# A DiT block on one core: where the sigmoid of the attention stage stands in ScalarE's order, and how one pair of modulation rows is ordered

## The chip, the cores and the metric

The kernel runs on one core of a Trainium2 chip. The metric is the device time of one execution in microseconds, the median of several runs. A core has five engines with an instruction stream each: TensorE (PE, matrix products), VectorE (DVE), ScalarE (ACT), GpSimd (POOL) and SyncE (SP, which here only issues transfers).

## What is computed

Two batches of 4096 rows of 512 numbers pass through one block with adaptive layer norms. Cut to what matters (the quantization rounds blocks of 16 numbers to an FP4 grid with a scale for each block):

```python
mod = (silu(c) @ wmod).reshape(2, 6, 1, -1)          # sa, ca, ga, sb, cb, gb
h = layernorm(x) * (1 + ca) + sa
xn = h / norm(h) * sqrt(d) * gamma
q, kv, a = split(xn @ W_qkva.T, 3)
a = sigmoid(a)
y[t] = a[t] * y[t-1] + kv[t]                         # scan along the rows
x = x + ga * (q * y)
h = layernorm(x) * (1 + cb) + sb
g, u = fp4_linear(h, w_gate), fp4_linear(h, w_up)    # 512 -> 1408
x = x + gb * fp4_linear(silu(g) * u, w_down)         # 1408 -> 512
```

## The kernel before

**Two stages.** The first (from line 778) does the gated scan and, beside it, the quantization of the three feed-forward weights. The second (from line 988) does the feed-forward part, 64 steps of 128 rows. Both have their order written out by hand: inside `tc.manual_schedule` each engine runs its instructions in the order in which the program issues them, so the order of the calls in the loop is the order on every engine's queue.

**The first stage** goes through 16 blocks of 512 rows (`NBLK`), each in four slots, one for each 128 of the 512 output features (`e`). Slot `s` stands for block `s // 4` and feature group `s % 4`; there are 64 slots and three more in which the last ones drain. The loop is at line 788. In a slot:

- TensorE runs `mix` (line 396): three products of 12 matmuls each (line 405) into three PSUM banks, in the order a, kv, q. Even slots use banks 0 to 2, odd ones 3 to 5. Operands are split in a high and a low half (`hl`), hence three passes.
- `gates` (line 415) takes the sigmoid of the product a on ScalarE, into the tile `sig`, which has one buffer. `scan` (line 420) runs along the rows on VectorE: it reads `sig` and the product kv, and writes `y`; ScalarE copies the last column to `cy` for the next block. `read_out` (line 430) multiplies by the product q. `halves` and `joined` (lines 437 and 446) split `y` for a transposing transfer and join it again, on ScalarE; `residual` (line 453) adds it to the rows on POOL and writes them to memory. All of these run a slot or more after `mix`: the loop keeps slot `s`'s products in `gate` and handles them in slot `s + 1`, `joined` and `residual` in slot `s + 3`.
- The rows of the next block are prepared, one group of 128 rows a slot: row group `g = slot + 4` is finished and `g + 1` begun. `norm_center` and `norm_shift` (VectorE, lines 166 and 172) apply the layer norm; `norm_square` (ScalarE, line 366) sums the squares, POOL makes the reciprocal root `rn` (`norm_gain`, lines 371 and 373); a slot later `norm_hi` (ScalarE, line 379) makes the high half and `norm_lo` (VectorE, line 384) the low half, and SyncE issues the transpose into `xT` (line 388). A block's first `mix` needs the four groups of its `xT`.
- Units of weight work, by the list `plan` (line 547), are loaded in one slot and handled in the next: the maxima of the weights' blocks in slots 6 to 22 (`weight_max`, line 479; two units a slot), their collection in 23 to 25, and their quantization in slots 26 to 59 (`quant`, line 97; one unit a slot, steps 1 to 6 spread over the slot). In the last slots the first row groups of the second stage get their statistics and quantization (`stats_x`, line 593; `quant_x`, line 606).

**ScalarE's order in a slot** is thus: the sigmoid of the slot before, `joined`, `norm_hi`, `cy`, `halves`, the unit's steps (among them `she` and `sle`), `norm_square` and the unit's first step.

**The opening** (`start`, line 659) is written out by hand too. The modulation rows are small products of two rows (`mod_rows`, line 230): each `s` of the pair gets its own 32 columns of the array by `tile_position`, and the k-steps of the `s` alternate. `start` calls it for the pair (1, 0) of batch rows at line 680, after two spread products (line 221) and before the first `mix`; the three others come in slot 10 (`MODS`), and are stored by `mod_store` (line 267) in slot 11.

Of the kernel before, what the change touches and what calls it, by code (L numbers as in the profile page):

```python
# [19 lines left out]
KC = D // P  # L20
# [23 lines left out]
def tile_adaln_block(  # L44
# [147 lines left out]
    wm = {}  # L192
# [34 lines left out]
            )  # L227
        return pm

    def mod_rows(*mods):  # L230

        pm = side((P, D))
        rows = [(s, slice(32 * n, 32 * n + B)) for n, s in enumerate(mods)]
        for k in range(KC):
            for s, at in rows:
                T.matmul(
                    pm[at, :],
                    sc[:, k, :],
                    wm[s][:, k, :],
                    start=k == 0,  # L240
                    stop=k == KC - 1,
                    tile_position=(0, at.start),
                )
        return pm, rows

    def mod_columns(s):
# [333 lines left out]
    mods = {}  # L580
# [78 lines left out]
    def start():  # L659
        a, b_, c_ = PARTS  # L660

        def load_mod_piece(s, k):
            S.dma_start(wm[s][:, k, :], wmod[k * P : (k + 1) * P, s * D : (s + 1) * D])

        load_mod(1, KC)
        norm_load(0)
        S.dma_start(gam, gamma.partition_broadcast(P))
        for k, then in enumerate((PARTS[0], PARTS[1], PARTS[2], None)):
            if then is None:
                norm_load(1)  # L670
            else:
                load_part(0, then)
            load_mod_piece(0, k)
        norm_load(2)
        norm_load(3)
        load_qkva(1)
        norm_load(KC)
        pc = mod_spread(1, 0)
        ps = mod_spread(0, 0)
        pair = mod_rows(1, 0)  # L680

        norm_moments(0)
        norm_stats(0)
        gamma_qkva(0, a, V)
        A.activation(ca[0], pc, AF.Copy, bias=1.0)
        square_qkva(0, a)
        gamma_qkva(0, b_, V)
        square_qkva(0, b_)
        inverse_qkva(0, a, a + 1)
        norm_center(0)  # L690
        gamma_qkva(0, c_, V)
        inverse_qkva(0, b_, b_ + 1)
        hi_qkva(0, a, True)
        square_qkva(0, c_)
        lo_qkva(0, a)
        inverse_qkva(0, c_, c_ + 1)
        hi_qkva(0, b_, True)
        norm_moments(1)
        norm_stats(1)
        lo_qkva(0, b_)  # L700
        A.copy(sa[0], ps)
        norm_center(1)
        hi_qkva(0, c_, True)
        norm_shift(0)
        norm_square(0)
        lo_qkva(0, c_)
        norm_gain(0, G)
        norm_shift(1)
        norm_square(1)
        norm_hi(0)  # L710
        norm_moments(2)
        norm_moments(3)
        norm_gain(1, G)
        norm_stats(2)
        norm_hi(1)
        norm_stats(3)
        norm_lo(0, xT)
        load_mod_piece(2, 0)
        norm_center(2)
        norm_shift(2)  # L720
        norm_square(2)
        norm_lo(1, xT)
        load_mod_piece(2, 1)
        load_part(2, a)
        norm_gain(2, G)
        norm_center(3)
        norm_shift(3)
        norm_square(3)
        norm_gain(3, G)
        norm_hi(2)  # L730
        gamma_qkva(1, a, V)
        norm_lo(2, xT)
        load_mod_piece(2, 2)
        load_part(2, b_)
        norm_hi(3)
        gamma_qkva(1, b_, V)
        square_qkva(1, a)
        square_qkva(1, b_)
        norm_lo(3, xT)
        load_mod_piece(2, 3)  # L740
        load_part(2, c_)
        norm_load(KC + 1)
        inverse_qkva(1, b_, a + 1)
        gamma_qkva(1, c_, V)
        mod_store(*pair)
        square_qkva(1, c_)
        hi_qkva(1, a, False)
        inverse_qkva(1, c_, c_ + 1)
        lo_qkva(1, a)
        hi_qkva(1, b_, True)  # L750
        norm_moments(KC)
        hi_qkva(1, c_, True)
        lo_qkva(1, b_)
        gamma_qkva(2, a, V)
        square_qkva(2, a)
        norm_stats(KC)
        lo_qkva(1, c_)
        norm_load(KC + 2)
        load_qkva(3)
        norm_center(KC)  # L760
        gamma_qkva(2, b_, V)
        square_qkva(2, b_)
        norm_shift(KC)
        norm_square(KC)
        norm_gain(KC, G)
        gamma_qkva(2, c_, V)
        square_qkva(2, c_)
        gain_qkva(0)
        norm_moments(KC + 1)
        inverse_qkva(2)  # L770
        norm_stats(KC + 1)
        for part in PARTS:
            hi_qkva(2, part, False)
            lo_qkva(2, part)
        gain_qkva(1)
        gain_qkva(2)
# [8 lines left out]
    with order:  # L785
        xT = new_xT()
        start()
        for slot in range(NS + 3):
            i, e = divmod(slot, KC)
            if e == 0 and slot < NS:  # L790
                if slot:
                    xT = nxT
                nxT = new_xT() if i + 1 < NBLK else None
            units, coming = coming, load_units(plan[slot]) if slot < len(plan) else []
            g = slot + KC
            if g + 3 < NT:
                norm_load(g + 3)
            cur = mix(i, xT, e) if slot < NS else None
            late = rows
            rows = None  # L800
            if slot == 0:
                cols = mod_columns(2)
            elif slot == MODS:
                rows = mod_rows(3, 4, 5)
            if gate is not None:
                gate = gates(*gate)
            if len(joining) == 2 or slot >= NS + 2:
                residual(*joined(*joining.pop(0)))
            if g < NT:
                norm_hi(g)  # L810
            if slot == 1:
                for part in PARTS:
                    square_qkva(3, part)
            if gate is not None:
                gate = scan(*gate)
            if slot == 1:
                signed_floor(gq, cols, atile([P, KC, B], F32, "mag"))
                prep_gain(0)
            if g + 2 < NT:
                norm_moments(g + 2)  # L820
            if gate is not None:
                gate = read_out(*gate)
            if g < NT:
                norm_lo(g, nxT)
            if gate is not None:
                joining.append(halves(*gate))
            if g + 2 < NT:
                norm_stats(g + 2)
            for u in units:
                u.advance(1)  # L830
            if g + 1 < NT:
                norm_center(g + 1)
            for u in units:
                u.advance(2)
                u.advance(3)
            if g + 1 < NT:
                norm_shift(g + 1)
                norm_square(g + 1)
            if slot == 1:
                scale_qkva(3)  # L840
                for part in PARTS:
                    hi_qkva(3, part, False)
                    lo_qkva(3, part)
            for u in units:
                u.advance(4)
            coming = [Unit(*c_) for c_ in coming]
            for u in coming:
                u.advance(0)
            if g + 1 < NT:
                norm_gain(g + 1, G)  # L850
            if slot == 0:
                for part in PARTS:
                    gamma_qkva(3, part, V)
            for u in units:
                u.advance(5)
                u.advance(6)
            assert all(u.step == 7 for u in units)
            if 0 < slot < KC:
                prep_gain(slot)
            if MODS - 5 <= slot < MODS - 2:  # L860
                load_mod(slot - MODS + 8)
            if late is not None:
                mod_store(*late)
            if slot == KC + 1:
                ca[1] = mod_load(1, 1, "mod_c1")
                sa[1] = mod_load(0, 1, "mod_s1")
            if slot == NS // 2 + KC:
                mods_for(0)
            if slot == NS // 2 + KC + 2:
                gbs[0] = mod_load(5, 0, "mod_gb")  # L870
            if slot in (NS - 6, NS - 5):
                for n in range(2):
                    n += 2 * (slot - NS + 6)
                    x1s[n] = load_x1(n)
            if NS - 5 <= slot < NS - 1:
                n = slot - NS + 5
                xst[n] = stats_x(x1s[n])
                if n in (1, 2):
                    run(quant_x(n - 1, x1s.pop(n - 1), xst.pop(n - 1)))
            gate = cur  # L880
# [190 lines left out]
```

## Time and profile before

| | us |
|---|---|
| median of 3 runs (1931.8 to 1933.85) | 1932.37 |
| the profiled execution | 1931.29 |
| its span, first to last instruction | 1929.5 |
| TensorE busy in the span | 1896.8 (98%) |
| VectorE busy | 1604.4 (83%) |
| ScalarE busy | 993.6 (51%) |
| POOL busy | 413.5 (21%) |

By stretch (busy us of each engine, granted clock of TensorE, mean share of the DMA engines):

| from, to | what | TensorE | VectorE | ScalarE | clock | DMA |
|---|---|---|---|---|---|---|
| 0 to 76.4 | opening, slots 0 to 3 | 57.36 | 53.61 | 36.08 | 0.89 | 0.84 |
| 76.4 to 244 | slots 4 to 23 | 159.75 | 130.31 | 83.97 | 1.00 | 0.78 |
| 244 to 555 | slots 24 to 63 | 311.00 | 283.84 | 230.78 | 1.00 | 0.91 |
| 555 to 1929.5 | second stage | 1368.65 | 1136.66 | 642.79 | 1.00 | 0.39 |

The lines of a profile are read so: in a timeline, start and length in us, the engine, the line of the kernel, the operation, what it writes and reads, how many; in brackets the idle time of the engine just before, and what ended it. "PEld" is the loading of weights into TensorE. In a list of waits: who waited for whom, the sum in us, how often, the longest. What ended a wait is inferred: where several conditions end close together, the last one is named.

### The profile page before, as it was taken

How to read it: one execution, taken by the hardware profiler on the slowest of the kernel's cores; microseconds unless marked ns; L12 is line 12 of the kernel's file. 1: busy time of each engine (PE TensorE's matmuls, PEld its weight loads, DVE VectorE, ACT ScalarE, POOL GpSimd, SP SyncE). 2: the span in 40 equal slices, each digit the busy share in tenths (PEclk: the TensorE clock that was granted, in tenths of full speed). 3: DMA queues.
4: the chain of work that ended last, by engine and by line, in shares of the span. 5: the costliest groups of instructions: out<-in, count | busy, mean ns of one | idle time of the engine just before them, and what ended most of it. 6: DMA issues, size and time to landing. Idle time of an engine off the chain costs nothing.

```text
span 1929.5 us, 25687 instructions
## 1 busy us (share of the span) xinstructions
PE 1896.8 (98%) x9220; PEld 899.4 (47%) x9220; DVE 1604.4 (83%) x2677; ACT 993.6 (51%) x1705; POOL 413.5 (21%) x597
## 2 busy tenths in 40 slices
PE   7899999999999999999999999999999999999999
PEld 4344444444444444444444444444444444444444
DVE  6778789999859988888888888878888888888865
ACT  4554577777755544444454445444544454444432
POOL 4544466666421010000000000001000000000000
PEclk8999999999999999999999999999999999999999
DMA  9796699999833444334433443344434333433333
GB/s 244 180 248 171 165 193 200 222 206 198 180 82 68 80 79 79 63 63 79 78 63 64 81 77 74 64 83 80 63 67 80 75 63 69 80 72 63 63 68 58
DMA packets 483202, 206.67 MB, mean 107 GB/s; under 512 B 439623, under 2 KB 440903, under 8 KB 483073
## 3 DMA queue, kind: packets, MB, share of 16 engines
q1 hardware_dynamic: 468624, 171.50, 41.9%
q0 software_dynamic: 14448, 33.52, 10.0%
q8 instruction: 72, 1.18, 0.3%
q14 instruction: 58, 0.47, 0.1%
HBM read 63.12 MB, written 33.58 MB: 50 GB/s over the span
## 4 chain that ended last, share of the span: by engine, by line
PE 84%; DVE 2%; issue 1%; ACT 1%; POOL 0%; DMA 0%; ACTq 0%; DVEq 0%; POOLq 0%
PE mm L898 46%; PE sd L945 24%; PE mm L405 15%; POOL xr L455 0%; DVE xn L122 0%; DVE ld L172 0%; DVE y L432 0%; DMA out_dram<-xr 0%; DVE y L423 0%; POOL out_dram L457 0%; DVE hl L125 0%; DVE ld L610 0%; DVE amx L147 0%; ACT she L113 0%; DVE hid L918 0%
## 5 line engine op out<-in xcount | busy, mean ns | idle before, releaser
L898 PEld LDWEIGHTS <-x2T 128*128 128x128 f16 x4608 | 450.9, 98 | 469.4 <-issue 1.3
L405 PE MATMUL mm<-xT,wqT 128*128 128x512 f16 (+1 forms) x2412 | 506.4, 374 | 21.0 <-DMA xT<-hl 12.6
L898 PE MATMUL mm<-wuT,x2T 128*128 128x512 f16 (+1 forms) x2304 | 487.7, 361 | 1.0 <-DVE hid L918 1.0
L898 PE MATMUL mm<-wgT,x2T 128*128 128x512 f16 (+1 forms) x2304 | 487.7, 361 | 0.0
L945 PE MATMUL sd<-wdT,hT 128*128 128x512 f16 x2112 | 465.8, 379 | 0.0
L405 PEld LDWEIGHTS <-wqT 128*128 128x128 f16 x2412 | 233.4, 100 | 294.8 <-issue 24.4
L945 PEld LDWEIGHTS <-hT 128*128 128x128 f16 x2112 | 206.6, 98 | 242.7
L913 ACT ACTIVATE silu<-mm,u 128x512 f32<-128x512 f32 (+1 forms) x192 | 125.1, 652 | 285.7 <-PE mm L898 281.9
L918 DVE SCALAR_TENSOR_TENSOR hid<-mm,u,silu 128x512 f32<-128x512 f32 (+1 forms) x192 | 128.4, 672 | 139.7 <-PE mm L898 130.6
L602 POOL TENSOR_SCALAR rstd<-vs 128x1 f32<-128x1 f32 x64 | 14.1, 221 | 983.9 <-ACT sq L600 983.9
L143 ACT ACTIVATE u<-ud,rms 128x1 f32<-128x1 f32 x64 | 19.0, 297 | 278.0 <-DVE rms L139 278.0
L120 ACT ACTIVATE sle<-sl 128x512 f16<-128x512 f32 (+2 forms) x162 | 147.2, 909 | 0.0
L113 ACT ACTIVATE she<-sh 128x1408 bf16<-128x1408 bf16 (+1 forms) x128 | 128.5, 1004 | 4.1
L969 POOL DMA_DIRECT2D out_dram<-o x63 | 56.2, 893 | 270.0 <-DVE o L963 266.1
L439 ACT COPY yh<-y 128x1024 uint16<-128x1024 uint16 x64 | 67.0, 1047 | 80.1 <-DVE y L432 70.7
L423 DVE TENSOR_TENSOR_SCAN y<-sig,cy,mm 128x512 f32<-128x512 f32 x56 | 71.6, 1279 | 43.3 <-POOL ss L371 19.3
L122 DVE SCALAR_TENSOR_TENSOR xn<-hid,xn 128x1408 f32<-128x1408 f32 x64 | 103.5, 1617 | 3.7 <-ACT hid L116 3.7
L106 DVE TENSOR_TENSOR xn<-hid,inv 128x1408 f32<-128x1408 f32 x64 | 104.0, 1625 | 2.2
L125 DVE SCALAR_TENSOR_TENSOR hhl<-hid,xn 128x1408 f16<-128x1408 f32 x64 | 104.0, 1625 | 2.2
L147 DVE TENSOR_REDUCE amh<-hid 128x88 f32<-128x1408 f32 x64 | 103.7, 1620 | 2.2
L116 ACT ACTIVATE hid<-xn 128x1408 f32<-128x1408 f32 x64 | 88.3, 1380 | 30.7 <-DVE xn L106 30.7
L455 POOL TENSOR_TENSOR xr<-xr,y 128x512 f32<-128x512 f32 x64 | 81.4, 1271 | 54.5 <-ACT y L447 53.7
(113 smaller groups left out, 1899.5 us busy)
## 6 DMA issues: line engine op xcount, KB each, us to landing
ld<-out_dram SPq DMA_DIRECT2D x65, 256.0 KB, 2.9
xr<-in_L_attn_x_dram SPq DMA_DIRECT2D x64, 256.0 KB, 3.4
out_dram<-xr POOLq DMA_DIRECT2D x64, 256.0 KB, 4.0
out_dram<-o POOLq DMA_DIRECT2D x63, 256.0 KB, 3.9
ld<-in_L_ffn_w_gate_dram SPq DMA_DIRECT2D x22, 256.0 KB, 3.2
ld<-in_L_ffn_w_up_dram SPq DMA_DIRECT2D x22, 256.0 KB, 3.2
ld<-in_L_ffn_w_down_dram SPq DMA_DIRECT2D x16, 256.0 KB, 3.0
scratch<-in_L_wmod_dram SPq DMA_DIRECT2D x12, 256.0 KB, 4.6
```

The costliest lines, as they stand in the source:

```text
L106: V.tensor_tensor(blocks(xn), blocks(src), spread(inv, nb), ALU.mult)
L113: A.activation(blocks(she), spread(sh, nb), AF.Copy, scale=WPEAK)
L116: A.activation(a, xn, AF.Abs, scale=MAGIC)
L120: A.activation(blocks(sle), spread(sl, nb), AF.Copy, scale=WPEAK)
L122: V.scalar_tensor_tensor(out=xn, in0=a, scalar=FLOOR, in1=xn, op0=ALU.max, op1=ALU.add)
L125: V.scalar_tensor_tensor(out=nq, in0=a, scalar=FLOOR, in1=xn, op0=ALU.max, op1=ALU.subtract)
L147: V.tensor_reduce(am, src.rearrange("p (b k) -> p b k", k=QB), AX.X, ALU.max, apply_absolute_value=True)
L405: T.matmul(pp[:, t : t + width], wqT[:, wp * KC + k, r * P : (r + 1) * P], xT[:, xp * KC + k, t : t + width], start=n == 0, stop=n == 3 * ...
L898: T.matmul(pp[:, : n1 - n0], x2T[:, xp * KC + k, :], wt[:, wp * KC + k, n0:n1], start=n == 0, stop=n == 3 * KC - 1,)
L913: A.activation(sl[:, :w], pairs[j][0][:, :w], AF.Silu, scale=u[:, 0:1])
L918: V.scalar_tensor_tensor(out=hid[:, n0:n1], in0=pairs[j][1][:, : n1 - n0], scalar=u[:, 1:2], in1=sl[:, : n1 - n0], op0=ALU.mult, op1=ALU.mult,
L945: T.matmul(pd, hT[:, hp * IC + k, :], wdT[:, wd_chunk(wp, k), :], start=n == 0, stop=n == 3 * IC - 1,)
```

## The change

`mod_rows` gets a switch that runs all k-steps of one row set before those of the next; only the opening's call uses it. In the loop, the sigmoid stays where it was up to slot 4. From slot 4 on (`KC` is 4) the sigmoid of the slot's own products is issued in that same slot, after steps 2 and 3 of the units and ahead of `norm_shift` and `norm_square` of the next rows; the next slot finds it done. In slot 4 both places are used, the old one for slot 3's products.

```diff
-    def mod_rows(*mods):
+    def mod_rows(*mods, one_by_one=False):
 
         pm = side((P, D))
         rows = [(s, slice(32 * n, 32 * n + B)) for n, s in enumerate(mods)]
-        for k in range(KC):
-            for s, at in rows:
-                T.matmul(
-                    pm[at, :],
-                    sc[:, k, :],
-                    wm[s][:, k, :],
-                    start=k == 0,
-                    stop=k == KC - 1,
-                    tile_position=(0, at.start),
-                )
+        steps = [(k, *r) for k in range(KC) for r in rows]
+        if one_by_one:
+            steps = [(k, *r) for r in rows for k in range(KC)]
+        for k, s, at in steps:
+            T.matmul(
+                pm[at, :],
+                sc[:, k, :],
+                wm[s][:, k, :],
+                start=k == 0,
+                stop=k == KC - 1,
+                tile_position=(0, at.start),
+            )
         return pm, rows
...
-        pair = mod_rows(1, 0)
+        pair = mod_rows(1, 0, one_by_one=True)
...
-            if gate is not None:
+            if gate is not None and slot <= KC:
                 gate = gates(*gate)
...
             for u in units:
                 u.advance(2)
                 u.advance(3)
+            if slot >= KC and cur is not None:
+                cur = gates(*cur)
             if g + 1 < NT:
                 norm_shift(g + 1)
                 norm_square(g + 1)
```

## Prediction

> **What bounds the kernel now.** TensorE is busy for 98% of the span, so only time in which it has no work can be won. I first ask where that is: the timeline of TensorE alone, with what ended each pause, and the chain of waits for the undisturbed rate.
>
> ```profile
> 76.41 31.24 PE L405 MATMUL mm<-xT,wqT 128*128 128x512 f16 x144 [2.56 <-DMA xT<-hl]
> 108.58 23.48 PE L405 MATMUL mm<-xT,wqT 128*128 128x512 f16 x108 [0.93 <-DMA xT<-hl]
> 131.99 3.61 PE L236 MATMUL sd<-scratch,sc 128*2 128x512 f32 x24
> 135.53 39.02 PE L405 MATMUL mm<-xT,wqT 128*128 128x512 f16 x180
> 176.58 31.24 PE L405 MATMUL mm<-xT,wqT 128*128 128x512 f16 x144 [2.02 <-issue]
> 210.43 31.24 PE L405 MATMUL mm<-xT,wqT 128*128 128x512 f16 x144 [2.62 <-DMA xT<-hl]
> 243.95 16.35 PE L405 MATMUL mm<-xT,wqT 128*128 128x512 f16 x75 [2.28 <-ACT y L447]
> ```
> ```profile
> 243.95 280.00 PE mm L405 x1296
> ```
>
> A slot is 36 matmuls, and 1296 in 280.00 us make 0.216 us each, 7.78 us a slot, 31.11 a block of four. Slot 4 starts at 76.41, slot 8 at 108.58, slots 16, 20 and 24 at 176.58, 210.43 and 243.95. All pauses stand where a block begins, and after 243.95 there is none until one of 1.03 us at 587. So slots 4 to 23 are short of something that isn't TensorE. Next I read one such boundary, slot 15 to 16, in the timeline of all engines:
>
> ```profile
> 172.01 0.74 DVE L384 SCALAR_TENSOR_TENSOR hl<-ld,rn,hl 128x512 f16<-128x512 f32 x1
> ...
> 172.82 1.29 SPq L388 DMA_TRANSPOSE xT<-hl  x1
> ...
> 175.85 0.74 DVE L172 SCALAR_TENSOR_TENSOR ld<-ld,rstd,sa 128x512 f32<-128x512 f32 x1
> 176.58 31.24 PE L405 MATMUL mm<-xT,wqT 128*128 128x512 f16 x144 [2.02 <-issue]
> 176.69 0.63 ACT L366 ACTIVATE sq<-ld 128x512 bf16<-128x512 f32 x1 [3.51 <-DVE ld L172]
> ...
> 177.32 0.67 ACT L417 ACTIVATE sig<-mm,us 128x512 f32<-128x512 f32 x1
> ...
> 178.08 1.28 DVE L423 TENSOR_TENSOR_SCAN y<-sig,cy,mm 128x512 f32<-128x512 f32 x1 [1.48 <-POOL ss L371]
> ```
>
> TensorE starts the block 3.76 us after SyncE issued the last transpose into xT (3.96 and 3.93 at the next two boundaries, so "issue" and "y L447" name the same wait), and that issue follows VectorE's norm_lo. VectorE sets the pace: scan to scan is 8.50 us, 0.72 more than TensorE's slot. In each slot it is idle for 1.48 us ahead of the scan: shift, then ScalarE's square, then the sigmoid behind it in ScalarE's order (177.32 + 0.67 = 177.99), then the scan at 178.08. ScalarE itself had idled 3.51 us ahead of the square, and the sigmoid's product was long there. The list of waits between 76 and 245 us adds them up:
>
> ```profile
> DVE y L423 <- POOL ss L371: 19.3, 13, 1.5
> ...
> DVE y L423 <- ACT sig L417: 7.1, 5, 1.5
> ```
>
> POOL's ss is no operand of the scan and ended at 177.73; it is the sigmoid in both lines, 18 waits of 1.48.
>
> [...] the sigmoid, ready, starts only after the square. [...] Here the granted clock is 0.50 between 25 and 30 us, behind a pause of 4.72. [...] 16 passes of the opening pair take 3.60 us, a pair of them each 0.43 us, and the spread rows' full-array passes take 0.43 each.
>
> **The change, part by part.**
> **1. The sigmoid ahead of the square, slots 4 to 24.** Nothing is added; 0.67 us of ScalarE goes from behind the square into the 3.51 us of idleness ahead of it. The scan can follow the shift at once, so VectorE's slot becomes 8.50 - 1.48 = 7.02 us. What is late next: norm_hi. Square, POOL's two operations and hi take some 2.5 us from the square's start, against 2.4 from the scan to norm_lo: 0.15 us more, 7.17 us. That is below 7.78, so TensorE becomes the bound and the pauses go. Then read_out starts 0.1 us after the product's end, norm_lo 0.65 later, the transpose's issue 0.81 later, its landing 3.95 later: 5.5 us into a slot of 7.78, 2.3 to spare.
> Start to start, the blocks took 176.58 - 135.53 = 41.05 (180 matmuls: 38.89), 33.85 and 33.52 (31.11 each): excess 2.16 + 2.74 + 2.41 = 7.31 us, all taken as won. Slot 8's excess is 32.17 - 31.11 = 1.06, but there the transpose was issued at 101.78 and landed 6.8 us later, behind a modulation load and three tiles issued from 98.77 on. Norm_lo comes only 0.5 us sooner (read_out then waits for the product's end, 99.75). Bounds 0 and 1.06; I take 0.2.
> **2. The wait that is added.** The sigmoid of slot s now stands on ScalarE from mid-slot until the first third of slot s's product is there, 2.6 us into it. Behind it: square, and through it POOL's ss and rn, norm_hi, norm_lo and the transpose. But norm_lo stands behind read_out of the whole product, 5.2 us later, so the wait can't be the last. It bites in slot 11: the modulation rows delay its product by 3.54, the square by some 1.5, and with it the copies of mod_store and VectorE. VectorE is then 1.9 us late at slot 12 and gains 0.6 a slot: level by slot 15. At nothing; cover gone, up to 1.5 us. `sig` has one buffer, but the scan that frees it is earlier in the same slot.
> **3. Slots 26 to 59.** VectorE needs 7.56 to 7.78 us a slot here and the scan hardly waits (L129 ends at 350.98, the scan starts at 351.03). The sigmoid falls between she/sle and the square, which starts 0.1 to 0.5 later; the two steps of a unit that VectorE does next don't need it. No gain, no loss.
> **4. The end of the stage, slots 59 to 63.** The sigmoid now precedes the statistics and quantization of the first rows on ScalarE. In slot 60 these start at 525.79 today; behind a sigmoid that waits until 526.7 for its third of the product and takes 0.6 they start at 527.3, 1.45 later with a small overlap. In slot 61 the third is there (534.4), and 0.6 is added. It is caught up before the last scan, which waits for TensorE anyhow:
>
> ```profile
> 552.56 1.28 DVE L423 TENSOR_TENSOR_SCAN y<-sig,cy,mm 128x512 f32<-128x512 f32 x1 [4.33 <-PE mm L405]
> ```
>
> 2.05 against 4.33: nothing. Cover gone, 2.05 us. The gap of 1.03 at 587 stays. No DMA issue and no POOL instruction is moved in its queue.
> **5. The opening pair one by one.**
>
> ```profile
> 16.93 3.60 PE L236 MATMUL sd<-scratch,sc 128*2 128x512 f32 x16
> 25.25 6.98 PE L405 MATMUL mm<-xT,wqT 128*128 128x128 f16 x72 [4.72 <-DMA xT<-hl]
> ```
>
> No tile runs beside another now: 16 x 0.43 = 6.9 us, ending at 23.8 in place of 20.5, ahead of xT at 25.25, 1.4 us to spare. The clock may then stay full from 25 us on; the rows after that wait for their own xT at 33.60 and 36.14, and the product of slot 3 waits 4.13 us for wqT at 63.19. So neither a faster start nor up to 2 us of a slower one counts: 0, bounds -0.3 and +0.5.
>
> **Sum.** 7.31 + 0.2 = 7.5 us. The profiled execution took 1931.29 us, its span 1929.5 and 1.8 around it: 1923.8. It lies 1.08 below the median of 1932.37; from the median, **1924.8 us**.
>
> **The rivals.**
> A. *The transposes land late.* With 167.6 us of that stretch at a DMA share of 0.78 squeezed into 160, the share is 0.82, and landing could take slot 8's 6.8 us in place of 3.95: 0.1 + 0.65 + 0.81 + 6.8 = 8.36, 0.58 over the slot at three boundaries. 1.75 us lost: 1926.6. Against it: between 300 and 500 us the share is 0.98 and TensorE never pauses.
> B. *The end of the stage shows* (part 4 without its cover): 2.05 lost, 1926.9.
> C. *It does not do what it says*: POOL releases the scan, as the list of waits has it, and VectorE stays at 8.50: 1932.4. Against it: ss ends 0.35 before the scan starts, the sigmoid 0.09.
> D. *Slower: VectorE becomes the bound in slots 26 to 59.* Its shortest slot is 7.56, 0.22 under TensorE's. If the sigmoid, put ahead of the square, delays VectorE by more than 0.22 + 7.5/34 = 0.44 us a slot, 34 slots eat the gain. Its whole 0.67 passed on would be 34 x 0.45 = 15.3, net 7.8 slower: 1940. For it: VectorE is 97% busy there. Against it: norm_hi of the next slot has idle room, as in part 3.
>
> **How the numbers follow.** Likeliest 0.68 (own range 1922.9 to 1926: all of slot 8's excess and the gap of 1.03 won at one end), A 0.13, B 0.08, C 0.06, D 0.05. Range 1922.9 to 1927.9, which leaves out C, D and the tail of B. 0.2% is 3.9 us, about what a measurement of this kernel can tell from no change. Likeliest, A and B are faster, 0.89; C the same, 0.06; D slower, 0.05.
>
> **What would show it.** Right: slots 16, 20 and 24 starting 31.1 us apart without a pause, slot 16 38.9 us after slot 11, the scan's 1.48 waits gone in slots 5 to 23, waits of VectorE for TensorE in their place, the span to slot 24 7.5 us shorter, and everything after it merely shifted. Wrong: pauses for xT still at the boundaries (A), a pause over 1.03 us around 580 (B), 1.48 still ahead of the scan under another name (C), pauses of TensorE between 244 and 520 us (D), or a first product later than 25.3.

## The result and the profile after

The changed kernel takes **1926.4 us** (median of 9 runs, 1925.1 to 1928.68); the kernel before, beside it on the same chip, 1933.57 (9 runs, 1931.8 to 1934.45). The ratio is 0.9966, with an interval of 0.9955 to 0.9976, so between 4.6 and 8.7 us are won. (One of the 13 runs of an experiment below, e2_pair_only, took 2001.41 us at a granted clock of 0.947 and is not among those that its ratio compares.)

The profiled execution took 1928.68 us, the slowest of the nine, with a span of 1926.9. Against the profiled execution of before (1931.29) only 2.6 us show. Three terms make them up, and the first two differ in sign, so the timeline of TensorE has to be read in parts. In the kernel after, two lines were added ahead of `mix`, so its matmul is L407, and the other lines up to the loop are two further down as well:

```profile
77.70 32.93 PE L407 MATMUL mm<-xT,wqT 128*128 128x512 f16 x144 [3.62 <-DMA xT<-hl]
111.43 23.48 PE L407 MATMUL mm<-xT,wqT 128*128 128x512 f16 x108 [0.80 <-DMA xT<-hl]
...
138.39 39.02 PE L407 MATMUL mm<-xT,wqT 128*128 128x512 f16 x180
177.65 84.53 PE L407 MATMUL mm<-xT,wqT 128*128 128x512 f16 x389 [0.24 <-issue]
```

The pauses of 2.02, 2.62 and 2.28 us ahead of slots 16, 20 and 24 are gone; 0.24 is left at slot 16, and this view shows none after it. With the second stage's first matmul at 551.11 (554.85 before), the terms are, from start to start:

| stretch | before | after | difference |
|---|---|---|---|
| up to slot 8 | 108.58 | 111.43 | +2.85 |
| slots 8 to 10 | 26.95 | 26.96 | 0 |
| slots 11 to 15 | 41.05 | 39.26 | -1.79 |
| slots 16 to 63 | 378.27 | 373.46 | -4.81 |
| the pause early in the second stage | 1.03 | 2.17 | +1.14 |

The stretch that the change aims at, slot 8 to the end of the stage, is 6.59 us shorter. The 2.85 ahead of it are the opening of this one execution: slot 4 starts 1.3 us later, after a pause of 3.62 in place of 2.56, and its block of 144 matmuls takes 32.93 in place of 31.24, at a granted clock of 0.79 between 76 and 84 us (1.00 before). In the experiments below the start of slot 8 moves between 108.4 and 112.5 us.

What VectorE waits for now is told by the list of waits between 76 and 245 us:

```profile
DVE y L434 <- ACT cy L428: 12.4, 14, 0.9
...
DVE y L425 <- PE mm L407: 6.9, 4, 3.9
...
DVE y L425 <- ACT sig L419: 1.2, 1, 1.2
```

The 18 waits of 1.48 ahead of the scan have become one of 1.2. But only 4 waits of the scan for TensorE took their place. There are 14 new ones of 0.88 ahead of `read_out` (L434). The timeline of all engines around one of them, slot 13's products:

```profile
158.25 0.68 ACT L419 ACTIVATE sig<-mm,us 128x512 f32<-128x512 f32 x1
...
161.68 1.27 DVE L425 TENSOR_TENSOR_SCAN y<-sig,cy,mm 128x512 f32<-128x512 f32 x1
...
162.49 1.15 ACT L449 COPY y<-yt 128x1024 uint16<-128x1024 uint16 x1
...
163.58 0.72 ACT L381 ACTIVATE hl<-ld,rn 128x512 f16<-128x512 f32 x1
...
164.21 0.18 ACT L428 COPY cy<-y 128x1 f32<-128x1 f32 x1
164.42 0.75 DVE L434 SCALAR_TENSOR_TENSOR y<-mm,gq,y 128x512 f32<-128x512 f32 x1 [0.88 <-ACT cy L428]
...
169.59 1.27 DVE L425 TENSOR_TENSOR_SCAN y<-sig,cy,mm 128x512 f32<-128x512 f32 x1
```

The sigmoid is ready at 158.93, and the scan follows the shift without a wait. `read_out`, however, writes over the `y` whose last column ScalarE's small copy `cy` reads, so it must come after that copy. `cy` takes 0.18 us, but stands in ScalarE's order behind the square, the copy of `joined` (1.15) and `norm_hi` (0.72). VectorE's slot is 169.59 - 161.68 = 7.91 us: 0.59 less than before, not 1.48 less. From the scan at 185.40 on most slots are shorter, 7.71 to 7.76 (8.30 to 8.35 before). Over the ten slots from 153.78 to 232.06 the mean is 7.83 (8.42 before), so VectorE and TensorE, whose slot is 7.78, run almost level.

### The profile page after: what moved, and what is told of

The parts are those of the page before. It is cut to its first block, busy times and chain, and to the rows that moved or that the text cites. A ratio compares the mean times of both kernels' runs of the same rounds, so it can differ in the third digit from the quotient of the medians.

```text
span 1926.9 us, 25653 instructions
## 1 busy us (share of the span) xinstructions
PE 1897.6 (98%) x9220; PEld 898.6 (47%) x9220; DVE 1604.6 (83%) x2677; ACT 997.3 (52%) x1705; POOL 413.7 (21%) x597
## 4 chain that ended last, share of the span: by engine, by line
PE 92%; DVE 3%; DMA 1%; ACT 1%; issue 1%; POOL 1%; SPq 0%; ACTq 0%; POOLq 0%; DVEq 0%
PE mm L902 46%; PE sd L949 24%; PE mm L407 22%; DMA scratch<-in_L_attn_W_qkva_dram 1%; DMA xT<-hl 1%; DVE hl L330 0%; POOL xr L457 0%; DVE y L434 0%; DVE ld L172 0%; POOL rs L303 0%; ACT sq L299 0%; DVE xn L122 0%; PE sd L238 0%; ACT yh L441 0%; DVE hl L324 0%
## 5 line engine op out<-in xcount | busy, mean ns | idle before, releaser
L407 PE MATMUL mm<-xT,wqT 128*128 128x512 f16 (+1 forms) x2412 | 506.1, 373 | 15.6 <-DMA xT<-hl 11.3
L407 PEld LDWEIGHTS <-wqT 128*128 128x128 f16 x2412 | 232.4, 99 | 290.1 <-issue 21.6
L106 DVE TENSOR_TENSOR xn<-hid,inv 128x1408 f32<-128x1408 f32 x64 | 104.0, 1625 | 2.2
L122 DVE SCALAR_TENSOR_TENSOR xn<-ld,xn 128x512 f32<-128x512 f32 (+1 forms) x98 | 67.0, 683 | 28.9 <-ACT ld L116 28.7
```

The costliest lines, as they stand in the source:

```text
L106: V.tensor_tensor(blocks(xn), blocks(src), spread(inv, nb), ALU.mult)
L122: V.scalar_tensor_tensor(out=xn, in0=a, scalar=FLOOR, in1=xn, op0=ALU.max, op1=ALU.add)
L407: T.matmul(pp[:, t : t + width], wqT[:, wp * KC + k, r * P : (r + 1) * P], xT[:, xp * KC + k, t : t + width], start=n == 0, stop=n == 3 * ...
```

## The experiments

Theory T: the place of the sigmoid ahead of the square is the whole gain; TensorE becomes the bound; `cy`'s wait takes some of the margin; the end of the stage gives about 1 us back. Rivals: the pair's order has a part in it (P), a transfer holds what is left (A), the end of the stage costs the 2 us that were priced (B), and VectorE is what limits slots 26 to 59 (D). Each diff is against the changed kernel, and every kernel computes the whole reference. All were timed in five rounds beside the kernel before; medians of different groups may be compared through the ratios only.

| kernel | us | ratio to before | interval | slot 8 starts | slot 8 to second stage | pause in second stage |
|---|---|---|---|---|---|---|
| before | 1933.57 | 1 | | 108.58 | 446.27 | 1.03 |
| the change | 1926.4 | 0.9966 | 0.9955 to 0.9976 | 111.43 | 439.68 | 2.17 |
| e1_sig_only | 1925.81 | 0.9957 | 0.9945 to 0.997 | 108.58 | 439.77 | 1.84 |
| e2_pair_only | 1933.63 | 0.9997 | 0.9988 to 1.0005 | 109.51 | 446.36 | 1.02 |
| e5_after_square | 1937.19 | 1.0018 | 1.001 to 1.0026 | 112.51 | 447.37 | 1.85 |
| e6_slots_4_25 | 1926.27 | 0.9963 | 0.995 to 0.9975 | 110.10 | 438.83 | 1.01 |
| e4_tail_old | 1925.76 | 0.9957 | 0.9943 to 0.997 | 110.35 | 439.01 | 1.01 |
| e3_cy_first | 1961.35 | 1.014 | 1.0126 to 1.0154 | 110.41 | 475.92 | 1.88 |
| e9_hi_after_cy | 1926.24 | 0.9968 | 0.9955 to 0.998 | 108.41 | 438.77 | 1.89 |
| e7_mods_late | 1926.23 | 0.9962 | 0.995 to 0.9975 | | | 1.74 |
| e8_all | 1924.02 | 0.9954 | 0.9941 to 0.9966 | | | 1.02 |
| e10_all_pair | 1925.08 | 0.996 | 0.9946 to 0.9973 | | | 1.02 |

The last three columns are from the one profiled execution of each. Where the two columns on slot 8 are empty, it follows slot 7 without a pause and has no start of its own in the view.

**e1_sig_only: the sigmoid alone.** The pair alternates again.

```diff
-        pair = mod_rows(1, 0, one_by_one=True)
+        pair = mod_rows(1, 0)
```

> The sigmoid moved as in the change, the opening pair left alternating. Theory (all of the gain is the sigmoid's, the pair is hidden behind the wait for xT at 25 us): the same time as the whole change, 1926 us give or take 1.5, ratio to before about 0.996; the stretch from the start of slot 8 to slot 24 takes 128.5 us as with the whole change (135.4 before). Rival (the pair one by one costs in the opening, where the changed kernel's profile is 1.3 us late at slot 4 and 2.9 us late at slot 8): 2 to 3 us faster than the whole change, about 1923.5, with slot 8 starting near 108.6 again.

**e2_pair_only: the pair alone.** The sigmoid is at the old place in all slots.

```diff
-            if gate is not None and slot <= KC:
+            if gate is not None and not (99 <= slot - 1 < 99):
...
-            if slot >= KC and cur is not None:
+            if 99 <= slot < 99 and cur is not None:
```

> The pair one by one, the sigmoid where it was. Theory: no change, ratio 1.000 within 0.001; slots 8 to 24 take 135.4 us with pauses of 2.0, 2.6 and 2.3 us at slots 16, 20 and 24. Rival (the pair costs in the opening): 1.5 to 3 us slower than before, 1935 to 1936.5, all of it before slot 8. What the clock does differs too: after the shorter pause ahead of the first product it should stay full at 25 us.

TensorE's timeline of e1_sig_only, and below it that of e2_pair_only:

```profile
135.54 126.82 PE L407 MATMUL mm<-xT,wqT 128*128 128x512 f16 x586
```
```profile
177.76 31.24 PE L407 MATMUL mm<-xT,wqT 128*128 128x512 f16 x144 [2.28 <-issue]
211.54 31.24 PE L407 MATMUL mm<-xT,wqT 128*128 128x512 f16 x144 [2.54 <-DMA xT<-hl]
245.06 17.21 PE L407 MATMUL mm<-xT,wqT 128*128 128x512 f16 x79 [2.29 <-DMA xT<-hl]
```

The sigmoid alone runs from slot 11 on without a pause up to the end of this view and has the whole gain. The pair alone keeps all three pauses, at 0.9997. P falls: the pair has no part in the gain.

**e5_after_square: the same slot, the other side of the square.** The sigmoid is issued in its own slot, as in the change, but behind `norm_shift` and `norm_square`. This parts "earlier by a slot" from "ahead of the square".

```diff
-            if slot >= KC and cur is not None:
-                cur = gates(*cur)
             if g + 1 < NT:
                 norm_shift(g + 1)
                 norm_square(g + 1)
+            if slot >= KC and cur is not None:
+                cur = gates(*cur)
```

> The change, with the sigmoid still in its own slot but behind norm_shift and norm_square. Theory (what was won is the place ahead of the square, which waits for the shift; the slot in which it is issued is nothing): the scan waits 1.48 us again in slots 5 to 23, pauses of 2 to 2.7 us at slots 16, 20 and 24, the time of before, 1933 to 1934. Rival (what was won is that the sigmoid no longer stands at the start of the slot, ahead of joined): the time of the change, 1926.

In its timeline the scan has its wait back, again with POOL's name on it, and in TensorE's timeline the pauses are back (the one ahead of slot 20 is short, but slot 16's block before it took 1.69 us longer):

```profile
191.18 1.28 DVE L425 TENSOR_TENSOR_SCAN y<-sig,cy,mm 128x512 f32<-128x512 f32 x1 [1.48 <-POOL ss L373]
```
```profile
181.25 32.93 PE L407 MATMUL mm<-xT,wqT 128*128 128x512 f16 x144 [2.76 <-issue]
214.97 31.24 PE L407 MATMUL mm<-xT,wqT 128*128 128x512 f16 x144 [0.79 <-DMA xT<-hl]
248.82 13.54 PE L407 MATMUL mm<-xT,wqT 128*128 128x512 f16 x62 [2.62 <-ACT y L449]
```

Scan to scan is 8.50 us, as before the change. So the place relative to the square is what matters, and POOL's `ss` is only the name that the inference gives (rival C): in e1_sig_only and the change `ss` and the square stand as they did, and the wait is gone. It came out slower than the 1933 to 1934 us that were expected, and at 1.0018 even slower than the kernel before. The profile's 5.8 us over that kernel are 3.9 up to slot 8, 1.1 in the stage and 0.8 in the second stage's pause; why its opening is so late (5.32 us of pause ahead of slot 4) wasn't tried.

**e6_slots_4_25 and e4_tail_old: where the gain lies, and what the end gives back.** e6 uses the new place in slots 4 to 25 only, e4 in slots 4 to 58 (`KC <= slot < NS - 5`), so that both have the old order at the end of the stage, and e6 also in the quantization.

```diff
-            if gate is not None and slot <= KC:
+            if gate is not None and not (KC <= slot - 1 < 26):
...
-            if slot >= KC and cur is not None:
+            if KC <= slot < 26 and cur is not None:
```

> The change for slots 4 to 25 alone; from slot 26 on, where weights are quantized, the sigmoid is at its old place. Theory (all is won in slots 5 to 23, nothing in the quantization, about 1 us lost at the end of the stage): 1925.5, as with the end of the stage undone, with a pause of 1.03 us in the second stage. Rival (the new place also helps or hurts VectorE in the 34 slots of quantization): over 1 us away from that.

> The change up to slot 58 only; from slot 59 on the sigmoid is back at its old place. Theory (the sigmoid ahead of the statistics delays slots 60 to 62 by some 2 us, the last but one yh is copied late, its transpose holds the last yh, and the pause in the second stage's second step grows from 1.03 to 2.17 us): the pause is 1.03 again and the kernel 1.1 us faster than the change. Rival (the longer pause comes from the stage's being early against the transfers): the pause stays at about 2.2 us and the time is that of the change.

Slot 8 to the second stage takes 438.83 and 439.01 us in these two: 7.44 and 7.26 less than before, so the whole gain lies in slots 11 to 25, and the quantization gives or takes nothing (D falls). Both have the old pause in the second stage, here in the timeline of e4_tail_old and, below, of the change:

```profile
581.64 2.75 PE L902 MATMUL mm<-wuT,x2T 128*128 128x512 f16 x12 [1.01 <-DVE hid L922]
```
```profile
528.21 1.45 POOL L457 TENSOR_TENSOR xr<-xr,y 128x512 f32<-128x512 f32 x1 [2.32 <-ACT y L449]
528.57 1.37 DVE L129 TENSOR_TENSOR hl<-hl,she 128x512 f16<-128x512 f16 x1
...
546.37 1.05 ACT L441 COPY yh<-y 128x1024 uint16<-128x1024 uint16 x1
...
548.82 1.28 DVE L425 TENSOR_TENSOR_SCAN y<-sig,cy,mm 128x512 f32<-128x512 f32 x1 [2.77 <-PE mm L407]
...
553.29 1.05 ACT L441 COPY yh<-y 128x1024 uint16<-128x1024 uint16 x1 [4.24 <-DMA yt<-yh]
...
584.55 2.75 PE L902 MATMUL mm<-wuT,x2T 128*128 128x512 f16 x12 [2.17 <-DVE hid L922]
```

The last scan still waits for TensorE (2.77), so VectorE's delay is hidden there, as the prediction said. The delay leaves by another door. `yh`, the tile that ScalarE fills for the transfer of `y`, has one buffer. Its copy for slot 62 comes at 546.37, 4.74 us ahead of the second stage, where it was 6.59 ahead before (548.26 against 554.85): 1.85 late. Besides, its transfer takes 5.75 us to land, against 3.56 before and 3.58 in e4_tail_old. (Close behind it, by 0.58, POOL issues its write of 256 KB, which takes 5.42; before, the write was issued 0.65 ahead of it and took 3.14. Whether the two slow each other wasn't tried.) So it lands 2.08 us after the second stage's start, where it landed 1.96 ahead of it before, and the copy for slot 63 has to wait for it until 553.29, 2.18 after that start; before it waited only for `read_out` and came 1.03 after (in e4_tail_old too). That is 1.15 us, and the transfer into `x2T` that stands at its end is issued 18.77 after the stage's start, 17.63 before: 1.14. The pause grew by 1.14. So B is half true: the landing moved by 4.04 us, and some 3 of them were covered, the time from the landing to slot 63's copy before. The copy's 1.85 alone would by this sum have been hidden.

The first two lines show where part of the 1.85 comes from. In slots 60 and 61 POOL's sum now starts just ahead of L129, a step of the quantization on VectorE, where it started just behind it before; L129 takes 1.37 us in place of 0.42 in both (more on this in the last section). Scan to scan these slots take 12.12 and 10.15 us, 10.00 and 9.00 before.

In the timed runs this doesn't stand out: 0.9957 and 0.9963 lie within the interval of the change.

**e3_cy_first: the new wait taken away by moving `joined` and `residual` behind the scan.** Of those two and `norm_hi`, then only `norm_hi` stands ahead of `cy`.

```diff
-            if len(joining) == 2 or slot >= NS + 2:
-                residual(*joined(*joining.pop(0)))
             if g < NT:
                 norm_hi(g)
...
                 gate = scan(*gate)
+            if len(joining) == 2 or slot >= NS + 2:
+                residual(*joined(*joining.pop(0)))
```

> The change, with joined and residual issued after the scan, so that ScalarE copies cy ahead of joined's copy of 1.15 us. Theory (read_out waits 0.88 us for cy, because cy reads the column of y that read_out overwrites, and cy stands behind joined and norm_hi; this makes VectorE's slot 7.90 us, just over TensorE's 7.78): the waits of read_out for cy vanish, VectorE waits for TensorE in slots 13 to 23, no pause at slots 16 and 20; 0.3 to 2 us faster than the change. Rival (the 7.90 us is set by another chain, such as norm_hi's, which the move doesn't shorten): scan to scan stays at 7.9 us, same time as the change.

By the ratios it is some 34 us slower than the change, and not even the wait was gone: `norm_hi` had to wait for POOL's `rn` (1.00 us), and `cy` behind it left `read_out` waiting 0.87 to 0.88 in slots 13 to 23. The cost is elsewhere. The timeline of e3_cy_first around one unit's `xn` (L106), and below it that line in the change:

```profile
353.80 1.66 POOL L457 TENSOR_TENSOR xr<-xr,y 128x512 f32<-128x512 f32 x1 [2.07 <-ACT y L449]
...
354.34 1.67 DVE L106 TENSOR_TENSOR xn<-ld,inv 128x512 f32<-128x512 f32 x1
```
```profile
350.91 0.66 DVE L106 TENSOR_TENSOR xn<-ld,inv 128x512 f32<-128x512 f32 x1
```

POOL's sum was moved with `joined` and now runs beside `xn`, which takes 1.67 us in place of 0.66 in most of the units. VectorE's slot becomes 8.40 to 8.46 us, above TensorE's 7.78, and TensorE pauses at almost every block. In slots 13 to 23 the sum runs beside `norm_center` instead, which takes 1.67 in place of 0.72, and the slot there is mostly 8.7 to 8.9. From slot 8 to the second stage 36.2 us are lost against the change, some 25 of them from slot 24 on (335.6 us from slot 24, 310.9 in the change). It shows that D's mechanism is real: some 0.65 us a slot on VectorE above TensorE's slot reaches the end here. The change just doesn't cause it.

**e9_hi_after_cy: the wait taken away with no move of POOL's work.** From slot 5 on `norm_hi` is issued behind the scan and its `cy`.

```diff
-            if g < NT:
+            if g < NT and slot <= KC:
                 norm_hi(g)
...
                 gate = scan(*gate)
+            if g < NT and slot > KC:
+                norm_hi(g)
```

> The change, with norm_hi issued after the scan from slot 5 on, so that ScalarE's order is joined, cy, norm_hi; joined and POOL's residual stay where they are. Theory (read_out's 0.88 us is cy waiting behind norm_hi, and the slowness of the earlier reordering came only from the residual's new place on POOL beside VectorE's xn): read_out's wait for cy falls to 0.3 us or less, VectorE's slot falls below 7.78 us, the scan or read_out waits for TensorE in slots 13 to 23, xn stays at 0.67 us, and the time is that of the change or up to 1 us less. Rival (any later norm_hi delays norm_lo and the transposes, and that is what made the earlier reordering slow): pauses of TensorE at block starts after 244 us and 10 us or more over the change.

The timeline of slot 13's products in e9_hi_after_cy:

```profile
157.76 1.27 DVE L425 TENSOR_TENSOR_SCAN y<-sig,cy,mm 128x512 f32<-128x512 f32 x1
...
159.61 0.18 ACT L428 COPY cy<-y 128x1 f32<-128x1 f32 x1
...
159.78 1.27 POOL L457 TENSOR_TENSOR xr<-xr,y 128x512 f32<-128x512 f32 x1 [0.16 <-ACT y L449]
159.83 0.75 DVE L434 SCALAR_TENSOR_TENSOR y<-mm,gq,y 128x512 f32<-128x512 f32 x1 [0.21 <-ACT cy L428]
160.49 1.10 DVE L386 SCALAR_TENSOR_TENSOR hl<-ld,rn,hl 128x512 f16<-128x512 f32 x1
...
165.36 1.27 DVE L425 TENSOR_TENSOR_SCAN y<-sig,cy,mm 128x512 f32<-128x512 f32 x1
```

The wait is 0.21 in place of 0.88. `norm_lo` takes 1.10 in place of 0.74 beside POOL's sum, so 0.36 comes back, and scan to scan is 7.60. With that VectorE is ahead of TensorE: its scan and `read_out` wait 13 times for products, ScalarE's sigmoid 14 times, and TensorE has no pause from slot 11 on. The last transpose for slot 16 is issued 5.00 us ahead of the slot's start (169.22, 174.22), those for slots 20 and 24 6.0 and 6.1; in the change they are issued 3.85, 3.90 and 3.95 ahead, as in the kernel before (3.76, 3.96, 3.93), so that TensorE just takes them as they land. Slot 8 to the second stage takes 438.77, 7.50 less than before and 0.91 less than in the change. So little doesn't show in the timed runs (0.9968).

**e7_mods_late: the modulation loads after slot 8's transposes.** Three loads of modulation weights are moved from slots 5 to 7 to slots 7 to 9.

```diff
-            if MODS - 5 <= slot < MODS - 2:
-                load_mod(slot - MODS + 8)
+            if MODS - 3 <= slot < MODS:
+                load_mod(slot - MODS + 6)
```

> The change, with the three modulation loads of 1 MB issued in slots 7, 8 and 9 in place of 5, 6 and 7. Theory (the transpose that slot 8 waits for lands 6.8 us after its issue because a modulation load and three tiles stand ahead of it in the transfers): it lands 4 to 5 us after its issue, slot 8's pause of 0.8 us goes, the block of slots 4 to 7 takes 31.2 us when the clock is full; 0.5 to 1.0 us faster than the change. Rival (it is norm_lo that comes late): the pause stays.

In its timeline of TensorE slots 4 to 10 are one run of 252 matmuls:

```profile
78.10 56.24 PE L407 MATMUL mm<-xT,wqT 128*128 128x512 f16 x252 [3.72 <-DMA xT<-hl]
```

The pause of 0.80 ahead of slot 8 is gone, with a transpose that lands 3.1 us after its issue (some 7 in the change): it belonged to the transfers, as the prediction took it. One of 0.25 stands ahead of slot 24. From 0.5 to 1.0 us were expected; the ratio, 0.9962, doesn't show them.

**e8_all and e10_all_pair: everything that helped.** e8 puts e9, e4 and e7 together and lets the pair alternate; e10 is the same with the pair one by one.

```diff
-        pair = mod_rows(1, 0, one_by_one=True)
+        pair = mod_rows(1, 0)
...
+            if g < NT and slot > KC:
+                norm_hi(g)
...
+            if KC <= slot < NS - 5 and cur is not None:
...
+            if MODS - 3 <= slot < MODS:
+                load_mod(slot - MODS + 6)
```

> What the runs point to, together: the sigmoid in its own slot for slots 4 to 58 only, norm_hi behind the scan from slot 5 on, the modulation loads in slots 7 to 9, the opening pair alternating. Theory: no pause of TensorE from slot 4 to the end of the stage, then the one of 1.03 us; the change less about 1 us (end of the stage) less 0.8 (slot 8): 1924 to 1925, ratio to before 0.995 to 0.996. Rival (the spread of the opening, some 2 us from run to run, hides these): the time of the change, 1926.

> The same with the pair one by one, as a second test of the pair. Theory (the pair is worth nothing either way): the same time as the alternating one, within 1 us. Rival (after the pair one by one the opening's products run sooner, wait longer for wqT and xT, and the clock is halved over the start of slot 4, as in six of eight profiles so far): 1.5 to 2 us slower than the alternating one.

At 1924.02 e8 is the lowest median of all, but its interval (0.9941 to 0.9966) overlaps that of the change, and the two weren't timed together: that it beats the change isn't shown. e8 and e10, which were timed together, lie 1.06 us apart with overlapping intervals.

## Why the prediction was right, point by point

**The bound and the mechanism were right.** The pauses of TensorE were VectorE's 8.50 us slot, and the sigmoid behind the square was what made it so (e1, e2, e5). Rival C is refuted by e5 and the change, D by e6 against e4.

**The sum was near, in part by luck.** 7.5 us were taken as won and 7.17 measured, median to median (the kernel before came out at 1933.57 beside the change, not at 1932.37). 1926.4 lies just beyond the likeliest case's own range and 0.2 from rival A's 1926.6, but A's mechanism isn't there. Two errors came out small: VectorE has none of the margin that part 1 gave it, and it is luck that its 7.83 lies so close to 7.78; and of the delay that part 4 put at nothing, 1.14 us came through.

**Part 1, the size of the gain: right to 0.8 us.** 7.31 us were taken as won between slot 8 and the second stage; 6.59 were in the change's profile, 6.50 in e1's, and 7.26, 7.44 and 7.50 in those of e4, e6 and e9. In e1, 0.66 us of what is missing is one pause, at 361.87, for a transpose. In the change 0.82 is missing at the starts of slots 16, 20 and 24, whose first matmuls come 0.40, 0.26 and 0.16 late. There the transposes are issued too late for any slack, and e9, which takes `cy`'s wait away, has none of this: so it is that wait which used up the margin. What it costs then hangs on how late VectorE comes into the stretch. e1, e4 and e6 have the wait too and miss only 0.05 to 0.24 at these starts; slot 11's scan stands 7.84 to 8.02 us behind the start of slot 11 there, 8.46 in the change. Why it is later in the change wasn't tried. Slot 8, of which 0.2 was taken, gave 0.13 in the change's profile (a pause of 0.80, 0.93 before).

**The term that was mis-sized is "what is late next": 0.15 us were taken for `norm_hi`; 0.88 was measured, and for `cy`.** The step followed the chain through the square and POOL to `norm_hi` and `norm_lo`, and left out the copy of one column that stands behind `joined` and `norm_hi` and guards the tile that `read_out` overwrites. So VectorE's slot became 7.83 on the mean, not 7.17, and it stayed 0.05 above TensorE's 7.78. The prediction held because that rest is so small: over the dozen slots of this stretch it comes to some 0.6 us, by this estimate. Had TensorE's slot been 7.2, some 0.6 us a slot would have been missing.

**Part 2, the added wait: right in its place, wrong in how it fades.** The timeline of the change shows the sigmoid of slot 11's product a:

```profile
141.25 0.69 ACT L419 ACTIVATE sig<-mm,us 128x512 f32<-128x512 f32 x1 [2.32 <-PE mm L407]
```

It waited 2.32 us for the product, and the square behind it started at 142.44. VectorE was to gain back 0.6 us a slot and be level by slot 15; at 7.91 a slot it gains nothing there. Slots 11 to 15 took 39.26 us, 0.37 more than their 38.89.

**Part 3, slots 26 to 59: right** (e4 and e6 within 0.2 us of one another).

**Part 4, the end of the stage: the cover was only half there.** The delay was 1.85 at slot 62's copy (2.05 was priced), and the scan's wait did hide it on VectorE. That the two are so close is luck: slots 60 and 61 lost 3.27 us, 1.9 of them in L129 beside POOL's sum, which the step didn't have, and slot 62 made up for 1.5. It is true that no POOL instruction was moved in its queue, but the sum moved against VectorE's work. The step also asked whether the last scan is late, not whether the one-buffer tile behind it is free, nor whether its transfer still lands as fast. 1.14 us came through in the change's profile, 0.7 to 0.9 in those of e1_sig_only, e7_mods_late and e9_hi_after_cy. The pause of over 1.03 us that was named as B's sign is there.

**Part 5, the pair: right.** It began at 17.42 in the change's profile and ended well ahead of the first `xT` at 25.68, and the clock between 24 and 30 us, whose staying full was the author's estimate, went from 0.53 to 1.00, behind a pause of 2.94 in place of 4.72; in e2, behind one of 2.98, it was 0.70 from 24 to 28 us. Nothing of a faster start reached slot 4, and e2's ratio is 0.9997. The sixteen passes took 5.32 us, not 6.9: by their starts four run alone, 0.43 us apart, then eight in pairs, then four alone, so tiles did still run beside one another. The first `xT` product came later than the 25.3 that was named as a sign of being wrong, but it waited 2.94 us for its transfer after the pair had ended.

**Rival A falls.** The stretch of 77.7 to 240 us did come to a DMA share of 0.82, as A had worked out, but the transposes into `xT` landed in a median of 3.8 us (3.7 before). The one late transpose found is that of e1 at 361.87.

**What stays open** is the opening. Slot 4 waits 2.56 and 2.82 us for its `xT` in the profiles of before and e1, 2.58 in that of e3, 3.05 to 3.82 in those of the change, e2, e4, e6, e7, e8, e9 and e10, and 5.32 in e5. In all but before, e1 and e9 (3.05) the block that follows takes longer: its 144 matmuls take 32.93 us, in e5 33.81, in place of 31.24, and the 252 up to slot 10 take 56.24 in e7, e8 and e10, against 31.24 + 23.48 in before. The granted clock, where it was read, was 0.79 from 76 to 84 us in the change and e8 and 0.60 from 76 to 80 us in e2, against 1.00 in before, e1 and e9. The longer block is in 8 of the 9 profiles with the pair one by one, and 1 of the 3 with it alternating (e8, with 3.70). So the order of the pair isn't needed for it; whether it makes it likelier, single profiles can't say. The timed runs of e2 bound what the pair's order costs with the old place of the sigmoid at 1.0 us (0.0005 of 1934); with the new place, e1 and e8 have the lower ratios (0.9957 against 0.9966, 0.9954 against 0.996), within the intervals.

## What to carry to other kernels

On an engine that works in order, as ScalarE did here (in the slot shown, `cy` started at 164.21, 1.26 us after the scan that it reads from had ended, behind `joined` and `norm_hi`), put an instruction ahead of one that waits for a slower partner, if its own operand is there sooner. When a wait is taken out, look for the next one not only along the data but along what an in-place write must wait for: a reader of 0.18 us that stands behind 1.9 us of other work is as good as a long one. And where a delay is called hidden, ask also which single buffer it holds at the end, and which instructions and transfers the new order lays side by side.

## What the runs showed of the hardware

**In these runs VectorE and POOL held each other up where each read two tiles of SBUF.** POOL's sum reads `xr` and `y`. In e3 it ends at 355.46 and `xn`, which reads `ld` and `inv`, 0.55 us later, at 356.01, though it takes 0.66 alone and had started at 354.34. In e9 the sum ends at 161.05 and `norm_lo`, which reads `ld` and `hl`, 0.54 later, after 1.10 us. In slots 60 and 61 of the change the sum (1.45) covers a step of the quantization (L129, which reads `hl` and `she`) which takes 1.37 in place of 0.42. `read_out`, which reads one operand from PSUM, keeps its 0.75 beside the same sum (164.42, in the slot shown). POOL pays too: in e3 its sum started at 353.80, while `norm_lo` still ran (353.59 to 354.33), and took 1.66 in place of 1.27. What in the core makes them wait for one another isn't shown.

**A block at a lower granted clock after a pause took 1.7 us or more longer.** A block of 144 matmuls takes 31.24 us after most pauses of 2.0 to 3.05 (granted clock 1.00 from 76 to 84 us in before, e1 and e9), 32.93 after those of 3.19 to 3.82 (0.79 from 76 to 84 us in the change), and 33.8 to 34.0 after 4.22 (e3) and 5.32 (e5). But it also takes 32.93 after one of 2.58 (e3, slot 4) and one of 2.76 (e5, at 181.25, with 0.83 from 180 to 190 us), and 34.12 after one of 2.98 (e3, the last block), while after 3.05 in e9 the clock stays at 1.00. So in these runs the length of the last pause alone doesn't decide.
